# VectorE's order fixed to the program's in the second image's last stage, and sets of convolution weights made in separated places of the first image

## The chip, the cores and the metric

The kernel runs on one core of one Trainium2 chip. The metric is the device time of one execution in microseconds (us). Before the change the median of three runs is 3011.64 us (3008.14 to 3016.84). In the program's names, PE is TensorE (matrix products), DVE is VectorE, ACT is ScalarE, POOL is GpSimd and SP is SyncE, which here only issues transfers (DMAs).

## The reference

Two images of 256 channels and 64 x 64 pixels pass through two layers, each added to its input after a group normalisation:

```python
x = x + _L0_conv_ref(_gn(x), L0_conv_qkv_w, L0_conv_qkv_b, 8)
x = x + _L1_conv_ref(_gn(x), ...)
```

Layer 0 is a plain attention of 8 heads over all 4096 pixels. Layer 1 is what the change touches. From q, k, v (1 x 1 convolutions of its input) it makes two attentions over groups of 64 pixels, one after the other ("lr" with widely spaced pixels, then "sr" with 8 x 8 blocks), and beside them a 3 x 3 convolution; the two results are added with the weights rate1 and rate2:

```python
feats = _bn_relu(_c1x1(ctx, lr_W_w), lr_W_scale, lr_W_shift)
qx = _bn_relu(_c1x1(_bn_relu(_c1x1(feats, sr_fq1_w), ...), sr_fq2_w), ...)
kx = _bn_relu(_c1x1(_bn_relu(_c1x1(feats, sr_fk1_w), ...), sr_fk2_w), ...)
ctx2 = _sa(qx, kx, vx, DH, DW)          # softmax(q k) v within a group of 64
feats2 = _bn_relu(_c1x1(ctx2, sr_W_w), sr_W_scale, sr_W_shift)
out_conv = lax.conv_general_dilated(f_conv, dep_w, (1, 1), ((1, 1), (1, 1)), ...)
return rate1 * out_att + rate2 * out_conv
```

## The kernel before

The program is one function, `direct_layers`, that works through image 0 and then image 1 (`b` is 0 or 1). The 4096 pixels of an image are 8 tiles of 512, and its 256 channels are 2 halves of 128 partitions. For each image come layer 0 (`project0`, `attention0`, most of the time) and then layer 1 in two parts, `layer1_first` (the "lr" attention) and `layer1_second` (the "sr" attention and the 3 x 3 convolution, the last stage of the image).

**The last stage.** `layer1_second` loops over the 8 tiles t. An iteration has, in the program's order: the q branch (`branch`: two products, phq L1582 and prq L1597, each followed by a ScalarE bn_relu, L1341, that makes hq and rq); a convolution step; the k branch in the same way (phk, prk, hk, rk); and `group_attention`: the scores sp (L1276), a softmax, two transposes at (L1308), a copy bd (L1317) and the products pc (L1328), with the values pvs (L1252) between them. The softmax is a chain of short VectorE operations with one exponential on ScalarE in its middle: the maximum nm4 (L1296), the difference e (L1298), the sum den (L1301), its reciprocal (L1302) and the scaled e (L1303). At the end of an iteration stand `conv_edges` (ScalarE, L1218), which corrects the tile's border pixels, and the result's additions. `spots` says which convolution steps lie in which iteration, at three places: 0 after the q branch, 1 within the attention (behind the scores, ahead of at), 2 after the attention.

**A step of the convolution.** The 3 x 3 convolution is done by small transforms, products of transformed weights with transformed pixels, and transforms back. Every call of `conv` makes the *transform* of the next step, col and v, and then runs the *step* itself, products and drain:

- In image 0 (`conv_transform`, `conv_step`, 16 steps (s, q)) GpSimd makes col (L1048) and v (L1052) alone. TensorE makes 32 products mm (L1062). The drain is a copy on ScalarE (L1069) and four VectorE operations z that read mm (L1070 to L1073). Additions into the tiles x follow (L1086, L1090, L1092).
- In image 1 (`wide_transform`, `wide_step`, 12 turns: (0,0) to (0,5), then (1,5) to (1,0)) GpSimd makes the first part of col (L1155), VectorE two scaled additions (L1157) and a last addition (L1160), and then GpSimd makes v in four operations (L1165). TensorE makes 32 products (L1180). The drain is a copy on ScalarE (L1198 for q = 1, L1200 otherwise) and four VectorE operations z (L1201 to L1204). Then 4 or 16 additions into the tiles xphase follow (L1211).

In both cases mm comes from a pool of one buffer (`pacc`), so a group of products can start only when the last drain operation of the group before is done. col has one buffer too.

**The wider weights.** Image 1 needs two more columns of transformed weights than image 0. `wider_weights(wf, r, stage)` makes them from image 0's weights `wf` for one of four rows r, called a set here. A set is four VectorE operations (L1102 to L1105, each 128 x 512) into `stage` and two transfers of 256 KB (L1107, issued by SP) from there to DRAM, from which image 1 loads them. `stage` is one tile, so a set can't be written before the transfers of the set before it are done.

**What sets the order.** Instructions of one engine run in the order in which they are emitted to it. Within `tc.manual_schedule(engines=...)` (L1612) the engines named keep the order of the program text. For the others a scheduler chooses the order by its own estimates of when operands are ready. `tc.issue_after(ins)` holds what is emitted under it behind the instruction `ins` on the engine of `ins` itself. `kept["bd"]` is the last bd copy, a VectorE instruction, and `kept["rows"]` is the last bn_relu of a hidden layer, a ScalarE instruction. `near` is true for the last two iterations of image 0, where TensorE and VectorE both keep the program's order; in all other iterations only TensorE does.

Of the kernel before, what the change touches and what calls it, by code (L numbers as in the profile page):

```python
# [41 lines left out]
def direct_layers(ctx: ExitStack, tc: tile.TileContext, a: dict, out: bass.AP, bad: bass.AP):  # L42
# [17 lines left out]
    def w4(shape, name, dtype=F32):  # L60
        return work.tile(shape, dtype, tag="w4", name=name)

    kept = {}
# [10 lines left out]
    def bank(shape, name, at=None):  # L74
        if at is None:
            at = psum["first"] + psum["turn"] % len(psum["banks"])
            psum["turn"] += 1
        return psum["banks"][at].tile(shape, F32, tag="bank", name=name)
# [52 lines left out]
    for name in ("w1", "w2"):  # L131
        by_out[name] = wpool.tile([P, KC, C], F32, tag="wp", name=f"{name}_by_out")

        for i in range(4):
            r = 64 * (i % 2)
# [63 lines left out]
    for u in range(4):  # L199
        r = HD0 * u  # L200
# [896 lines left out]
    def wider_weights(wf, r, stage):  # L1097

        parts = [stage[:, n, :].rearrange("p (k c) -> p k c", k=KC) for n in range(2)]
        one, two = parts  # L1100
        w = [wf[:, :, 4 * r + q, :] for q in range(4)]
        nc.vector.scalar_tensor_tensor(one, w[3], 4.0, w[0], ALU.mult, ALU.add)  # L1102
        nc.vector.tensor_sub(two, w[1], w[2])
        nc.vector.scalar_tensor_tensor(one, two, 2.0, one, ALU.mult, ALU.add)
        nc.vector.scalar_tensor_tensor(two, two, -4.0, one, ALU.mult, ALU.add)  # L1105
        for n in range(2):
            nc.sync.dma_start(out=wf_more[:, n, :, r, :], in_=parts[n])  # L1107
# [380 lines left out]
    def layer1_second(b, xts, feats, mean, rstd, shift, pacc, following):  # L1488
# [29 lines left out]
        wf = None  # L1518
# [9 lines left out]
        def conv(behind_products=None, behind_drain=None):  # L1528
            nonlocal done, wf
            if wf is None:  # L1530
                wf = fetch_conv_weights(b)
            if done + 1 < len(turns):
                ahead[done + 1] = transform(b, xp, *turns[done + 1])
            additions = step_of(b, xts, wf, ahead.pop(done), *turns[done], pacc, behind_products)
            next(additions)
            held.append(additions)
            if behind_drain:
                behind_drain()
            else:
                while held:  # L1540
                    next(held.pop(0), None)
            done += 1
# [18 lines left out]
        if b:  # L1561
            wf = WideWeights(b)
# [9 lines left out]
        for t in range(NT):  # L1572
            nt = f"sr_{b}_{t}"
            f = [
                feats[k][:, 8 * t : 8 * t + 8].rearrange("p o d e -> p (o d e)") for k in range(KC)
            ]

            def hidden(one, col1, nm):
                hid = w4([P, KC, T], f"h{nm}_{nt}")
                ph = [bank([P, T], f"ph{nm}_{nt}_{m}") for m in range(KC)]  # L1580
                for k, m in ((0, 0), (0, 1), (1, 0), (1, 1)) if t == 0 else ((0, 0), (1, 0), (0, 1), (1, 1)):
                    nc.tensor.matmul(  # L1582
                        ph[m], wts[one][:, k, m * P : (m + 1) * P], f[k], start=k == 0, stop=k == KC - 1
                    )
                    if k == KC - 1:
                        kept["rows"] = bn_relu(hid[:, m, :], ph[m], col1, m)
                return hid

            def branch(one, two, col1, col2, nm, between=None):
                hid = hids.pop(nm, None) or hidden(one, col1, nm)  # L1590
                if between:
                    between()
                res = w4([P, KC, T], f"r{nm}_{nt}")
                pr = [bank([P, T], f"pr{nm}_{nt}_{m}") for m in range(KC)]
                for k in range(KC):
                    for m in range(KC):
                        nc.tensor.matmul(  # L1597
                            pr[m], wts[two][:, k, m * P : (m + 1) * P], hid[:, k, :], start=k == 0, stop=k == KC - 1
                        )
                for m in range(KC):  # L1600
                    bn_relu(res[:, m, :], pr[m], col2, m)
                return res

            E = mybir.EngineType
            seam = b == 0 and t == NT - 1
            near = b == 0 and t >= NT - 2

            def step(n=1):
                for _ in range(n if near else 0):
                    next(then)  # L1610

            with tc.manual_schedule(engines={E.PE, E.DVE} if near else {E.PE}):  # L1612
                hids = {}
                if t == 0:
                    hids = {"q": hidden("fq1", V_FQ1, "q"), "k": hidden("fk1", V_FK1, "k")}
                q = branch("fq1", "fq2", V_FQ1, V_FQ2, "q")
                if pending:
                    next(pending)
                    next(pending, None)
                    pending = None  # L1620
                with tc.issue_after(kept["rows"].ins):
                    for tt in images.get(t, ()):
                        to_image(tt)
                if 0 in spots.get(t, ()) and (b or t > 2):
                    conv(step if seam else None)
                if seam:
                    for n in sorted(results):
                        give(n)
                k = branch("fk1", "fk2", V_FK1, V_FK2, "k", step if seam else None)
                in_x = b and t % 4 == 0  # L1630
                res = xpool.tile([P, KC, T], F32, tag="x", name=f"res_{nt}") if in_x else w4([P, KC, T], f"res_{nt}")

                def to_res(m, pc, res=res):

                    bn_relu(
                        res[:, m, :].rearrange("p (d o e) -> p o d e", d=8, o=8),
                        pc.rearrange("p (o d e) -> p o d e", o=8, d=8), V_SRW, m,
                    )

                parts = group_attention(  # L1640
                    nt, q, k, lambda c, w, f=f: f[c][:, w * P : (w + 1) * P], wts["fv"], to_res, apart=t + 1 < NT,
                    split=t + 1 == NT, fill=lambda m: step(3 if seam else 0),
                )
                if seam:
                    step(5)
                if b == 0 and t == 2:
                    conv(behind_drain=lambda: next(parts))
                else:
                    next(parts)
                step()  # L1650
                if 1 in spots.get(t, ()):
                    conv(None if t < 2 and b == 0 else lambda: next(parts))
                elif b or t > 1:
                    next(parts)
                if t < 2 and b == 0:
                    pending = parts
                else:
                    if seam:
                        step(2)
                    next(parts, None)  # L1660
                    if seam:
                        for _ in then:
                            pass
                if 2 in spots.get(t, ()):
                    conv(step)
            if b == 0 and t == 1:


                with tc.issue_after(kept["seam"]):
                    kept["bias"] = conv_weights()  # L1670
                with tc.issue_after(kept["made"].ins):
                    for k in range(KC):
                        nc.vector.memset(xp[:, k, 0, :], 0.0)
                ahead[0] = conv_transform(b, xp, *turns[0])
            for tt in ((), (0, 1))[t] if b == 0 and t < 2 else (t,):
                conv_edges(xts, tt)
            if b == B - 1 and t == 2:
                report()
            results[t] = res
            if b:  # L1680
                for m in range(KC):
                    nc.vector.tensor_scalar(res[:, m, :], res[:, m, :], wts["rate1"], None, ALU.mult)
            if b == 0 and t in (3, 4):
                if t == 3:
                    stage = xpool.tile([P, KC, T], F32, tag="x", name="stage")
                with tc.issue_after(kept["bd"].ins):
                    for r in range(2 * (t - 3), 2 * (t - 3) + 2):
                        wider_weights(wf, r, stage)
            for n in sorted(n for n in results if done >= (NQ * (n // 4 + 1) if b else 4 * (n // 2 + 1))):
                give(n)  # L1690
            if b == 0 and t == NT - 3:
                next(then)
# [625 lines left out]
```

## Time and profile before

| what | value |
|---|---|
| median of three runs | 3011.64 us (3008.14, 3011.64, 3016.84) |
| the profiled execution's own time | 3011.38 us |
| its span | 3009.5 us, 63901 instructions |
| mean TensorE clock granted | 0.995 of full speed |
| the part of image 0's last stage with the sets and the steps around them | about 1360 to 1480 us |
| last stage of image 1, with its convolution steps | about 2740 to 3009 us |

The profile is one execution; times in it count from the start of its span. A row of the timeline gives start, length, engine, line of the kernel, operation, and output tile <- input tiles; "x32" says that 32 instructions in a row are shown as one, and the brackets at the end give the idle time before them and what ended it. A row of the waits gives who waited <- for whom: the sum in us, the number of times, and the longest. A row of the windows gives a stretch, its length, the busy time and number of operations of PE, PE's weight loads, DVE, ACT and POOL, then the granted TensorE clock, the share of the DMA engines and GB/s. Matmuls are pipelined, so their lengths overlap a little.

### The profile page before, as it was taken

The page shows a single profiled execution, that of the slowest core. Times are in us where ns is not written, and L with a number is a line of the kernel's source. Part 1 is how long each engine was busy: PE and PEld are TensorE (multiplying, and loading weights), DVE is VectorE, ACT ScalarE, POOL GpSimd, SP SyncE. Part 2 cuts the span into 40 slices and gives each one's busy share as a digit, 9 for nine tenths or more (in the row PEclk, how much of TensorE's full clock was granted, in tenths as well). Part 3 has the DMA queues.
Part 4 walks back from the last instruction along what each step waited for, and adds up shares of the span by engine and source line. Part 5 has one row for each costly group of instructions (what it writes and reads, how often), then busy time and mean ns, then how long its engine had stood idle before and what let it go on. Part 6 is the DMA issues. An engine that isn't in the chain of part 4 may idle for free.

```text
span 3009.5 us, 63901 instructions
## 1 busy us (share of the span) xinstructions
PE 2945.0 (98%) x25043; PEld 1830.7 (61%) x25043; DVE 2499.7 (83%) x3196; ACT 2336.1 (78%) x3283; POOL 815.0 (27%) x910
## 2 busy tenths in 40 slices
PE   7999999999999999998999999999999999998998
PEld 4555556665565656676765565566655656566665
DVE  4698998999899999956655989989998989955874
ACT  2699999999999994532235999999999999943433
POOL 1022222322222221065400232223222222213430
PEclk9999999999999999999999999999999999999999
DMA  7979778897888761231249797788978877720010
GB/s 257 277 139 184 148 157 168 160 190 149 164 181 161 154 145 43 62 139 64 63 171 264 147 182 146 163 166 162 187 147 170 176 156 151 154 69 22 15 57 30
DMA packets 254660, 431.82 MB, mean 143 GB/s; under 512 B 99416, under 2 KB 118668, under 8 KB 252172
## 3 DMA queue, kind: packets, MB, share of 16 engines
q0 software_dynamic: 96960, 237.57, 41.2%
q1 hardware_dynamic: 157244, 189.81, 23.1%
q8 instruction: 198, 3.24, 0.4%
q14 instruction: 114, 0.93, 0.1%
q10 hardware_dynamic: 144, 0.26, 0.0%
HBM read 124.27 MB, written 70.48 MB: 65 GB/s over the span
## 4 chain that ended last, share of the span: by engine, by line
PE 86%; DVE 6%; DMA 4%; ACT 2%; POOL 1%; issue 1%; SPq 0%; ACTq 0%; POOLq 0%; DVEq 0%
PE ring L594 32%; PE av L609 30%; PE mm L1062 3%; PE mm L1180 3%; PE p_wk L457 2%; PE p_wq L457 2%; DVE prep L984 2%; PE pv L483 2%; PE prq_sr L1597 1%; PE prk_sr L1597 1%; PE phk_sr L1582 1%; PE phq_sr L1582 1%; PE pvs_sr L1252 1%; DMA acc<-v 1%; PE ring L609 1%; PE pvs_lr L1252 1%
## 5 line engine op out<-in xcount | busy, mean ns | idle before, releaser
L600 ACT ACTIVATE es<-ring 128x512 f32<-128x512 f32 (+2 forms) x1574 | 1201.5, 906 | 35.8 <-PE ring L594 21.3
L594 PE MATMUL ring<-q,k 128*128 128x512 f32 x4096 | 1082.8, 407 | 7.9 <-ACT es L600 5.1
L646 DVE TENSOR_TENSOR e<-e,es 128x1024 f32<-128x1024 f32 (+1 forms) x942 | 1029.0, 1153 | 28.5 <-ACT es L600 27.0
L594 PEld LDWEIGHTS ring<-q,k 128*128 128x128 f32 x4096 | 731.3, 188 | 382.6 <-ACT es L600 116.8
L600 ACT ACTIVATE v<-ring 128x512 f32<-128x512 f32 (+2 forms) x1036 | 785.1, 892 | 17.2 <-PE ring L594 7.7
L609 PE MATMUL av<-es,v 128*32 128x256 f32 (+1 forms) x9648 | 722.5, 389 | 0.0
L646 DVE TENSOR_TENSOR e<-e,v 128x1024 f32<-128x1024 f32 (+1 forms) x624 | 669.1, 1128 | 15.5 <-ACT v L600 15.0
L609 PE MATMUL av<-v 128*32 128x256 f32 x6224 | 506.1, 389 | 0.0
L609 PEld LDWEIGHTS av<-es,v 128*32 128x32 f32 x9648 | 325.1, 109 | 263.3 <-issue 104.5
L609 PEld LDWEIGHTS av<-v 128*32 128x32 f32 x6224 | 222.2, 109 | 169.9 <-issue 70.4
L656 POOL DMA_DIRECT2D es<-es x116 | 99.0, 854 | 442.1 <-ACT es L600 419.1
L656 POOL DMA_DIRECT2D acc<-es x126 | 126.8, 1011 | 130.6 <-ACT es L600 42.9
L654 POOL DMA_DIRECT2D es<-es x20 | 11.4, 570 | 495.3 <-ACT es L600 390.0
L656 POOL DMA_DIRECT2D es<-v x74 | 63.3, 856 | 291.0 <-ACT v L600 259.4
L1062 PE MATMUL mm<-v,wf 128*128 128x256 f32 x512 | 118.2, 391 | 10.6 <-DVE z L1073 10.6
L656 POOL DMA_DIRECT2D v<-es x114 | 116.2, 1019 | 25.6 <-ACT es L600 12.2
L1062 PEld LDWEIGHTS mm<-v,wf 128*128 128x128 f32 x512 | 99.5, 196 | 28.7 <-issue 14.5
L656 POOL DMA_DIRECT2D acc<-v x86 | 88.2, 1026 | 83.6 <-DMA acc<-es 37.8
L1052 POOL TENSOR_TENSOR v<-col 128x512 f32<-128x512 f32 x64 | 83.6, 1334 | 88.3 <-DVE x L1086 33.9
L1180 PE MATMUL mm<-v,wf 128*128 128x256 f32 x384 | 85.6, 381 | 2.6 <-issue 2.6
L984 DVE SCALAR_TENSOR_TENSOR prep<-prep 128x256 f32<-128x256 f32 x198 | 83.6, 477 | 0.4
L1165 POOL TENSOR_TENSOR v<-col 128x512 f32<-128x512 f32 x48 | 59.9, 1282 | 86.1 <-DVE col L1160 86.1
(281 smaller groups left out, 2790.2 us busy)
## 6 DMA issues: line engine op xcount, KB each, us to landing
acc<-es POOLq DMA_DIRECT2D x122, 512.0 KB, 6.2
acc<-v POOLq DMA_DIRECT2D x78, 512.0 KB, 6.4
es<-es POOLq DMA_DIRECT2D x136, 256.0 KB, 4.0
v<-es POOLq DMA_DIRECT2D x134, 256.0 KB, 5.2
k<-wk_halves SPq DMA_DIRECT2D x64, 512.0 KB
q<-wq_halves SPq DMA_DIRECT2D x256, 128.0 KB
v<-v POOLq DMA_DIRECT2D x88, 256.0 KB, 5.0
es<-v POOLq DMA_DIRECT2D x86, 256.0 KB, 4.2
```

Source lines behind the costliest of these rows:

```text
L457: made = nc.tensor.matmul(pq, w0[nm][:, k, g * P : (g + 1) * P], xn[:, k, n], start=k == 0, stop=k == KC - 1)
L483: nc.tensor.matmul(pv[:, j, :], xn[:, k, n0 : n0 + P], w0["wv0"][:, k, :], start=k == 0, stop=k == KC - 1)
L594: touch(nc.tensor.matmul(sc[:, i, :], held["k", g // 2][:, j * P : (j + 1) * P], held["q", g, u // 2][:, u % 2, :], start=True, stop=True, ...
L600: nc.scalar.activation(dst, sc, AF.Exp, scale=SC0), set(range(at % BANKS, at % BANKS + m))
L609: note(nc.tensor.matmul(dst[HD0 * u : HD0 * u + HD0, n], lhs, rhs(u)[:, n], start=start, stop=stop))
L646: nc.vector.tensor_add(dst[:, s, :], dst[:, s, :], src)
L656: nc.gpsimd.dma_start(out=dst, in_=src, accum_op=ALU.add)
L984: nc.vector.scalar_tensor_tensor(acc, src, s, acc, ALU.mult, ALU.add)
L1052: (nc.gpsimd.tensor_add if plus else nc.gpsimd.tensor_sub)(dst, rows(one), rows(two))
L1062: nc.tensor.matmul(mm[:, m, r, :], wf[:, k, 4 * r + q, m * P : (m + 1) * P], v[r // 2][:, r % 2, k, :], start=k == 0, stop=k == KC - 1,)
L1180: nc.tensor.matmul(mm[:, r, :, m, :], wide.of(q)[:, k, r, m * P : (m + 1) * P], v[r // 2][:, r % 2, k, :], start=k == 0, stop=k == KC - 1,)
L1252: nc.tensor.matmul(pv[:, i, :], tokens(c, 2 * half + i), wv[:, c, :], start=c == 0, stop=c == KC - 1)
```

## The change

Two things are changed in `layer1_second`. First, the iterations of image 1 now name VectorE beside TensorE in `tc.manual_schedule`, so that VectorE keeps the program's order there. Second, the four sets of wider weights: before, sets 0 and 1 were emitted after iteration t = 3 of image 0 and sets 2 and 3 after t = 4, each pair behind the last bd copy. Now sets 0, 1 and 2 are emitted after t = 3, 4 and 5, one each, behind the bd copy; set 3 is emitted within iteration t = 5, behind the step at place 0, under `tc.issue_after(kept["rows"].ins)`.

```diff
-            with tc.manual_schedule(engines={E.PE, E.DVE} if near else {E.PE}):
+            with tc.manual_schedule(engines={E.PE, E.DVE} if near or b else {E.PE}):
...
                 if 0 in spots.get(t, ()) and (b or t > 2):
                     conv(step if seam else None)
+                if b == 0 and t == 5:
+                    with tc.issue_after(kept["rows"].ins):
+                        wider_weights(wf, 3, stage)
...
-            if b == 0 and t in (3, 4):
+            if b == 0 and 3 <= t < 6:
                 if t == 3:
                     stage = xpool.tile([P, KC, T], F32, tag="x", name="stage")
                 with tc.issue_after(kept["bd"].ins):
-                    for r in range(2 * (t - 3), 2 * (t - 3) + 2):
-                        wider_weights(wf, r, stage)
+                    wider_weights(wf, t - 3, stage)
```

The first part adds and removes no instruction. The second keeps the sixteen VectorE operations and eight transfers and changes only where they stand.

## The prediction

> **What bounds the kernel now.** I read the page first, then TensorE's waits and timeline in the two places the diff touches, then the engines they wait for.
>
> ```profile
> PE 2945.0 (98%) x25043; PEld 1830.7 (61%) x25043; DVE 2499.7 (83%) x3196; ACT 2336.1 (78%) x3283; POOL 815.0 (27%) x910
> ...
> PE 86%; DVE 6%; DMA 4%; ACT 2%; POOL 1%; issue 1%; SPq 0%; ACTq 0%; POOLq 0%; DVEq 0%
> ```
>
> TensorE is busy 98% of the span and is 86% of the chain that ends last. The change moves work on VectorE, so it can only alter the few waits TensorE still has. The views of its waits, over 1340 to 1540 us (first image) and 2740 to 3010 us (second image):
>
> ```profile
> PE mm L1062 <- DVE z L1073: 9.6, 2, 7.0
> ```
> ```profile
> PE at_sr L1308 <- DVE e_sr L1303: 3.7, 1, 3.7
> PE mm L1180 <- issue: 2.6, 1, 2.6
> ```
>
> Its timeline shows the four (idle before, in brackets):
>
> ```profile
> 1381.03 8.83 PE L1062 MATMUL mm<-v,wf 128*128 128x256 f32 x32 [2.60 <-DVE z L1073]
> ...
> 1431.19 9.94 PE L1062 MATMUL mm<-v,wf 128*128 128x256 f32 x32 [7.04 <-DVE z L1073]
> ...
> 2769.59 0.69 PE L1308 MATMUL at_sr<-ident,e_sr 128*128 128x128 f32 x2 [3.74 <-DVE e_sr L1303]
> ...
> 2779.56 7.14 PE L1180 MATMUL mm<-v,wf 128*128 128x256 f32 x32 [2.60 <-issue]
> ```
>
> A group of 32 products undisturbed takes 7.07 (1366.21); at 1381 it took 8.83, at 1431 9.94. The stretches behind three of the idles say why; PEclk is the third figure from the end:
>
> ```profile
> 1381.00:1384.00 3.00, 2.97 (x10) 2.51 (x11) 2.99 (x11) 0.50 (x3) 0.00 (x0) 0.71 0.00 0
> 1431.00:1434.00 3.00, 2.81 (x7) 2.30 (x8) 1.89 (x8) 0.57 (x2) 1.03 (x1) 0.50 0.45 162
> 2769.50:2772.00 2.50, 2.41 (x7) 2.05 (x8) 2.46 (x5) 0.00 (x0) 1.12 (x1) 0.50 0.11 46
> ```
>
> So an idle costs itself and then some: 2.60+1.76=4.4 at 1381 (4.54 by the starts of neighbouring groups), 7.04+2.87=9.9 at 1431, 3.74+2.6 at 2769. After 2779 the clock stayed at 1.00. The price of half rate is thus 0 to 2.9.
>
> VectorE around the last one:
>
> ```profile
> 2778.14 0.73 DVE L1157 SCALAR_TENSOR_TENSOR col<-col,xp 128x544 f32<-128x544 f32 x1 [4.59 <-POOL col L1155]
> 2778.78 0.68 DVE L1204 TENSOR_TENSOR z<-z,mm 128x512 f32<-128x512 f32 x1
> ...
> 2803.10 8.13 DVE L1211 SCALAR_TENSOR_TENSOR xphase<-z,xphase 128x256 f32<-128x256 f32 x16
> ...
> 2924.34 5.54 DVE L1211 SCALAR_TENSOR_TENSOR xphase<-z,xphase 128x256 f32<-128x256 f32 x16
> ```
>
> The last drain of mm into z (L1204) stood behind a col operation that waited 4.59 for GpSimd; "issue" is really this, because the products share one PSUM tile. And the same 16 additions take 8.13 beside GpSimd's v and col (2798.93 to 2806.3), 5.54 without it: operations with two SBUF inputs advance about one per GpSimd operation (1.27 each). Drains from PSUM keep their 0.7.
>
> **First image: the sets.** A set is four operations L1102–1105 (0.69 each) and two transfers on SP. Before, two sets stand back to back at A (after t=3, mm at 1381) and at B (after t=4, mm at 1431); the second set of each waits for the first's transfers (1.57 at 1375.24). By the built order of the changed program, A keeps one set; B still has two, sets 1 and 3, since the wait on kept["rows"], a ScalarE result, does not hold VectorE's operations; the third place (C, after t=5) gets set 2. That is three places, not four.
> A: VectorE's first set ends at 1373.67, z then at about 1376.9, before TensorE is ready (1378.26): −4.5, all of it unless z is 1.4 later. The next claimant is mm itself, so no later wait is in sight.
> B: same sequence, 0; bounds −10 (sets fall apart in time) to +1.
> C: L1102 goes between L1070 and L1071 of the z at 1459.05 and is held by GpSimd's v until about 1460.6, so z ends 1.07 later, 0.4 past TensorE's readiness; the remaining three come before the z at 1470.12, done by about 1474.2 against 1475.3. Take +0.4 (0 to 2).
> SP: the two transfers of set 3 now stand ahead of one x load of the next image, needed far later; 0. Were that load wanted at once, it would come one write later; the nearest row for such a hold is the 1.57 that set waits for set, and none of TensorE's waits is on SP.
> Sum −4.1 (−14 to −1).
>
> **Second image: VectorE in program order.** The softmax chain (L1296–1303) now precedes the column operations (L1157, L1160) of the next turn, but the first or first two L1157 of each turn after that are still ahead of the drains' end: in program order transform(next) stands before the step of this turn. So the long wait goes, and each drain can wait for GpSimd anew. From the rows, with T the start of a turn's products when attention follows: softmax begins T+0.12; col on VectorE 2.36 later (2940.76 to 2943.22, less the overlap); GpSimd's v 2.76 after col begins (2828.83 to 2831.58); the next col 5.07 after v (2831.58 to 2836.65); its end 2.23 on. Thus the next L1157 may run at T+12.54, whereas the drain is ready at T+8.3.
> *Start.* mm_0_0 at 2758.68; e is done by 2761.3, so at follows at once (3.74+2.6 gone), and mm_0_1 starts at 2770.28 for 2779.56. But v for the second turn begins only at 2763.92, the third col gates VectorE (additions held, col 2772.55–2775.53), GpSimd's next col ends 2782.88, and the drain between ends 2788.23: mm_0_2 at 2788.35 for 2792.55, though TensorE is ready at 2783.2. Gain 4.2, of which a new idle of 5.15 is already taken off; its clock costs +2.6 (1.7 to 2.9, between the 1381 and the 1431 row). Net −1.6.
> *t=2.* The wait for rk (0.5 in all) goes: −0.5. The drain of mm_0_3 waits for L1157 until T+12.54, its additions start T+16.05, the edge operations (ScalarE, L1218) need the fifth of them at T+17.9, and in ScalarE's new order hq's second half now stands behind an edge pair. Before, hq did too, as here, but the additions were in time:
>
> ```profile
> 2822.63 0.49 ACT L1218 ACTIVATE xphase<-xphase,edges 128x8 f32<-128x8 f32 x2
> 2823.53 0.51 ACT L1218 ACTIVATE xphase<-xphase,edges 128x8 f32<-128x8 f32 x2 [0.41 <-DVE xphase L1211]
> 2823.95 0.76 ACT L1341 ACTIVATE hq_sr<-phq_sr,vecs 128x512 f32<-128x512 f32 x1
> ```
>
> hq ends T+19.07; prq's second half wants it at T+15.9: +3.25, clock +1.3 (0 to 2.6).
> *t=3.* Same shape at mm_0_5, two more additions needed: hq T+18.6 against T+16.46: +2.15, clock +0.5 (0 to 1.8).
> *t=4, 5.* The additions of turn (1,3) run beside v and col, so the softmax of t=4 begins 3.6 late (38.0 against 34.4 after turn (1,4) starts). The 7.1 of products cover that, but bd, which now follows col on VectorE, comes 0.8 late. The additions of turn (1,2) are held the same way, their first and fourth feed the edges ahead of hq of t=5, and prq waits 3.9: +4.7, clock +2.0 (0 to 2.6).
> *From t=6* no column work is left: 0; if a drain slipped past its 1.3 cover it would cost below 1.
> Sum: −1.6−0.5+4.55+2.65+6.7 = **+11.8**; the bounds are −9.5 (3.74, 2.62, 2.60 and 0.5 gone, nothing new) and +16 (every clock price at its upper end, 15.3, and 1 from t=6).
>
> [...] The idle of 2.60 at 1378.4 left 0.71 of the clock and lost 1.8, that of 3.74 left 0.50. [...]
>
> **Sum.** The profiled execution took 3011.38 (span 3009.5), 0.26 under the median 3011.64. 3011.38 −4.1 +11.8 = **3019.1**.
>
> **Rivals.**
> *New waits cost the full price* (slower): at each of the four new idles (mm_0_2, prq of t=2, 3 and 5) half rate costs 2.87 as at 1431, 11.5 for the 6.4 taken: 3024; with one wait's delay handed to the next, up to 3029. For: the new idles exceed 2 us each. Against: after 2779 it cost nothing. It decides once three of the four cost over 2.
> *The waits don't form* (not slower): one mechanism, GpSimd's col. If it is done by T+9 in place of T+12.5, the drains are not held, the last three waits fall away and 3005 remains (−4.1 −2.1); with the idle before mm_0_2 gone too, 2997.8 (−4.1 −9.5). For: col takes only 2.2 and before the change it was done long ahead. Against: v of 5.0 stands in front of it, and v waits for VectorE's col, which now comes after softmax.
> *The sets truly come apart*: B's 10 goes too, 3009 with the second image as summed. Against: the built order has them adjacent. That A's gain does not appear (change without effect there) would give 3011.38 +0.4 +11.8, 3024.
>
> **How the numbers follow.** The waits form about as summed: 0.50, own range 3013 to 3025, 0.28 of it within 0.3% (9 us, about what a measurement tells from no change), 0.22 above. Full price or more, or A without gain: 0.26, slower. Waits don't form: 0.17, 0.08 same and 0.09 faster. Sets apart: 0.07, same. So faster 0.09, same 0.43, slower 0.48. The range of 3005 to 3027 leaves out the 2998 end and the top of the full-price case, two in ten.
>
> **What would show it.** Right: no wait at the first image's mm after t=3; still about 7 before the one after t=4; no wait at the first at of the second image; a wait of about 5 at mm_0_2 with L1157 ahead of a drain; prq waits of 2 to 4 on hq, released by additions. Wrong: VectorE's L1157 never waiting for GpSimd in front of a drain, or ScalarE running hq ahead of the edges.

## The result and the profile after

The changed kernel takes 3017.17 us (median of 20 runs, 3013.75 to 3020.14), the kernel before 3011.54 us (20 runs, 3008.14 to 3016.84). The ratio is 1.0017 with a 95% interval of 1.0010 to 1.0023, so the change costs between 3 and 7 us. The forecast was 3019.1. The profiled execution of the changed kernel took 3017.19.

Its page, two lines:

```profile
span 3015.7 us, 63901 instructions
...
PE 2947.1 (98%) x25043; PEld 1829.6 (61%) x25043; DVE 2505.7 (83%) x3196; ACT 2336.2 (77%) x3283; POOL 815.8 (27%) x910
```

The busy times have hardly moved. What moved are TensorE's waits. The view of its waits over the same stretches as before, first image and second image (without two of 0.2 in the second):

```profile
PE mm L1062 <- DVE z L1073: 7.0, 1, 7.0
```
```profile
PE prq_sr L1597 <- ACT hq_sr L1341: 8.3, 3, 3.5
PE mm L1180 <- POOL v L1165: 5.2, 1, 5.2
```

Of the four waits before, three are gone (2.6 in the first image, 3.7 and 2.6 in the second). Four new ones stand in the second image, and the wait of 7.0 is untouched. TensorE's timeline:

```profile
1379.87 7.07 PE L1062 MATMUL mm<-v,wf 128*128 128x256 f32 x32
...
1428.28 9.99 PE L1062 MATMUL mm<-v,wf 128*128 128x256 f32 x32 [7.05 <-DVE z L1073]
...
2762.67 0.38 PE L1308 MATMUL at_sr<-ident,e_sr 128*128 128x128 f32 x2
...
2785.49 8.83 PE L1180 MATMUL mm<-v,wf 128*128 128x256 f32 x32 [5.15 <-POOL v L1165]
...
2822.99 3.54 PE L1597 MATMUL prq_sr<-hq_sr,wt_fq 128*128 128x512 f32 x4 [3.01 <-ACT hq_sr L1341]
...
2861.56 1.98 PE L1597 MATMUL prq_sr<-hq_sr,wt_fq 128*128 128x512 f32 x4 [1.82 <-ACT hq_sr L1341]
...
2932.31 5.40 PE L1597 MATMUL prq_sr<-hq_sr,wt_fq 128*128 128x512 f32 x8 [3.52 <-ACT hq_sr L1341]
```

The wait of 5.15 is put down to GpSimd's v, which had ended at 2777.6. The drain on VectorE had not. VectorE's timeline of the changed kernel shows it, and then the drain at t=2 and the additions at t=5:

```profile
2779.91 1.36 DVE L1157 SCALAR_TENSOR_TENSOR col<-col,xp 128x544 f32<-128x544 f32 x2 [7.15 <-POOL col L1155]
...
2784.55 0.69 DVE L1204 TENSOR_TENSOR z<-z,mm 128x512 f32<-128x512 f32 x1
...
2816.51 0.72 DVE L1157 SCALAR_TENSOR_TENSOR col<-col,xp 128x544 f32<-128x544 f32 x1 [3.58 <-POOL col L1155]
2817.15 0.68 DVE L1202 TENSOR_TENSOR z<-z,mm 128x512 f32<-128x512 f32 x1
...
2925.97 9.10 DVE L1211 SCALAR_TENSOR_TENSOR xphase<-z,xphase 128x256 f32<-128x256 f32 x16
```

At 2779.91 the column operation of the next iteration had waited 7.15 for GpSimd, and the drain behind it ended only at 2785.24, a quarter of a microsecond ahead of the products. At 2816.51 the same operation stands between the first and the second drain operation. At 2925.97 nothing waits in the queue, but the sixteen additions take 9.10 beside GpSimd's v and col, against 5.54 alone. GpSimd's timeline there:

```profile
2922.49 5.20 POOL L1165 TENSOR_TENSOR v<-col 128x512 f32<-128x512 f32 x4 [9.69 <-DVE col L1160]
2927.78 2.66 POOL L1155 TENSOR_TENSOR col<-xp 128x1088 f32<-128x1088 f32 x1
```

ScalarE's timeline of the changed kernel shows how that reaches prq at t=2, and at t=5 in the last row:

```profile
2821.77 0.51 ACT L1218 ACTIVATE xphase<-xphase,edges 128x8 f32<-128x8 f32 x2 [4.34 <-DVE xphase L1211]
2822.18 0.76 ACT L1341 ACTIVATE hq_sr<-phq_sr,vecs 128x512 f32<-128x512 f32 x1
...
2931.09 0.50 ACT L1218 ACTIVATE xphase<-xphase,edges 128x8 f32<-128x8 f32 x2 [3.33 <-DVE xphase L1211]
```

hq's second half stood behind a border correction that waited 4.34 for an addition; at t=5 both halves stood behind one that waited 3.33.

The gains and losses by place, from the starts of groups of products in the two profiled executions (us, minus is faster):

| place | forecast | measured |
|---|---|---|
| A, products after t=3 of the first image | −4.5 | −4.52 |
| B, products after t=4 | 0 | +0.07 |
| C, products after t=5 | +0.4 | +0.27 |
| second image, first to fourth turn's products | −1.6 | −2.28 |
| t=2, wait for rk | −0.5 | −0.51 |
| t=2, prq | +4.55 | +4.97 |
| t=3, prq | +2.65 | +1.92 |
| t=4 and 5 | +6.7 | +5.59 |
| from t=6 | 0 | 0.00 |
| sum | +7.7 | +5.5 |

The spans differ by 6.2, and 0.7 of it is not in the table. The changed kernel was already 1.6 late ahead of place A, 0.8 of it in the wait for the first transfer (14.9 for 14.1); it regained 0.4 between place C and the second image's first products, and 0.5 behind the last pc. What the change moves lies outside these stretches.

### The profile page after: what moved, and what is told of

Same layout as the page of the kernel before. It is cut to its first block, busy times and chain, and to the rows that moved or that the text cites. A ratio compares the mean times of both kernels' runs of the same rounds, so it can differ in the third digit from the quotient of the medians.

```text
span 3015.7 us, 63901 instructions
## 1 busy us (share of the span) xinstructions
PE 2947.1 (98%) x25043; PEld 1829.6 (61%) x25043; DVE 2505.7 (83%) x3196; ACT 2336.2 (77%) x3283; POOL 815.8 (27%) x910
## 5 line engine op out<-in xcount | busy, mean ns | idle before, releaser
L1062 PEld LDWEIGHTS mm<-v,wf 128*128 128x128 f32 x512 | 98.5, 194 | 26.1 <-issue 12.5
L1180 PEld LDWEIGHTS mm<-v,wf 128*128 128x128 f32 x384 | 73.7, 194 | 18.3 <-POOL v L1165 6.0
```

The lines of the kernel that those rows point to most:

```text
L1062: nc.tensor.matmul(mm[:, m, r, :], wf[:, k, 4 * r + q, m * P : (m + 1) * P], v[r // 2][:, r % 2, k, :], start=k == 0, stop=k == KC - 1,)
L1180: nc.tensor.matmul(mm[:, r, :, m, :], wide.of(q)[:, k, r, m * P : (m + 1) * P], v[r // 2][:, r % 2, k, :], start=k == 0, stop=k == KC - 1,)
```

## The experiments

Two lengths are used below to compare profiles: I, from the products of step (1,0) to those of step (3,0) in the first image, and II, from the first turn's products to the last pc of the second image. Before: I 121.5, II 239.6. Changed: I 117.3, II 249.3. Times and ratios are against runs of the kernel before on the same chip.

### One part alone: the sets

Only the second part of the change is made; line 1612 is left as before (`{E.PE, E.DVE} if near else {E.PE}`).

> Only the sets are moved; VectorE's order in the second image's last stage is left as in the kernel before. My theory (the two parts act in separate places and add up): 4.2 us faster than before (-4.5 at the products after t=3, +0.1 after t=4, +0.3 after t=5), about 3007.4, with the 7 us wait after t=4 still there and the second image's waits of 3.7 and 2.6 back. Rival (the gain in the first image is handed on to a later wait, or the two parts depend on each other): within 1.5 us of before.

Measured: 3008.81 against 3010.73, ratio 0.9994 (0.9985 to 1.0003). I is 116.5, II 239.7: the wait of 2.6 is gone, the 7.0 is there, the second image is as before. The interval reaches from 4.5 faster to 0.9 slower and so does not tell the theory from the rival. The same kernel was run once more:

> The first kernel of this study once more, only the sets moved, to narrow its interval (1.9 faster, between 4.5 faster and 0.9 slower). My theory (the wait of 2.6 goes; its clock costs between 0 and 1.8 from one execution to the next): 2.5 to 4.5 faster than before, 3 to be named. Rival (the gain is given back in the first image): under 1.5 faster.

Measured: 3007.68 against 3013.71, ratio 0.9986 (0.9977 to 0.9995), that is 1.5 to 6.9 faster, about 4, where the first run had about 2. The rival, under 1.5, stands at the very edge of this interval, so it is unlikely but not excluded; the forecast of 4.1 lies in both intervals. In the profiles, I is 116.5 and 116.0 for 121.5.

### The other part alone: the order

```diff
-            with tc.manual_schedule(engines={E.PE, E.DVE} if near else {E.PE}):
+            with tc.manual_schedule(engines={E.PE, E.DVE} if near or b else {E.PE}):
```

> Only VectorE's order is fixed; the sets stay in their two pairs. My theory: 9.7 us slower than before, about 3021.2: the gains of 16 at the start of the second image's last stage are outweighed by waits of 5.2 at the third turn's products, 3.0 and 1.8 at prq of t=2 and 3, and 3.5 at prq of t=5, each with up to 1.8 of lower clock behind it. Rival (the changed kernel's loss comes in part from the sets): below 3018.

Measured: 3020.87 against 3010.73, ratio 1.0040 (1.0028 to 1.0052). II is 249.7, 10.1 longer than before, with waits of 5.13, 3.01, 1.80 and 3.51. The loss lies wholly in this part. Within the intervals the two parts add up: this loss is 8 to 16, the gain of the sets about 2 and 4, and the whole change costs 3 to 7. This run also gave a surprise in the first image, where nothing had been changed. The view of the windows, over the first 3 us behind the wait of 2.61 (2.60 before), of this kernel:

```profile
1381.00:1384.00 3.00, 2.98 (x14) 2.66 (x15) 2.98 (x11) 0.52 (x3) 0.00 (x0) 1.00 0.00 0
```

The clock stayed at 1.00, where the profile before had 0.71 after the same wait, and the products behind it took 7.14 for 8.83. I is 119.1 in place of 121.5 with the same instructions. The price of this idle, 0.07 in one execution and 1.76 in the other, is not a constant of the program.

### The border corrections out of hq's way

```diff
+                if b and t == 0:
+                    with tc.issue_after(kept["rows"].ins):
+                        for tt in range(1, 5):
+                            conv_edges(xts, tt)
...
-            for tt in ((), (0, 1))[t] if b == 0 and t < 2 else (t,):
+            for tt in () if b and 0 < t < 5 else ((), (0, 1))[t] if b == 0 and t < 2 else (t,):
                 conv_edges(xts, tt)
```

> The changed kernel, with the border corrections on ScalarE (L1218) of tiles 1 to 4 of the second image emitted in iteration 0 in place of iterations 1 to 4; VectorE's instruction order is the changed kernel's. My theory (the three prq waits come about because hq's bn_relu stands behind border corrections that wait for late additions): all three waits go, 5.0+1.9+5.4 with their clock, so 12.3 faster than the changed kernel, about 3004.9; the wait of 5.2 at the third turn's products stays. Rival (prq waits because ScalarE or the products' results themselves are late, whoever stands before): the waits stay, 3017.

Measured: 3007.05 against 3010.73, ratio 0.9984 (0.9975 to 0.9992): 3.7 faster than before, where the changed kernel was 5.6 slower, so 9.3 for the 12.3 expected. II is 237.9, 11.3 shorter than the changed kernel's. Of TensorE's waits in the second image, only one is over 0.2:

```profile
PE mm L1180 <- POOL v L1165: 5.1, 1, 5.1
```

All three prq waits are gone while VectorE runs the very same order: a late drain or late additions cost TensorE nothing there as long as nothing of ScalarE's waits for them ahead of hq. Most of the 1.0 that II falls short of the forecast lies in the products behind the 5.13, which took 9.68 here, 8.83 in the changed kernel's profile.

### The columns held behind the drain

```diff
-        nc.vector.tensor_sub(z1, z1, products(3))
+        kept["drain"] = nc.vector.tensor_sub(z1, z1, products(3))
...
-                ahead[done + 1] = transform(b, xp, *turns[done + 1])
+                with tc.issue_after(kept["drain"].ins) if b and done else ExitStack():
+                    ahead[done + 1] = transform(b, xp, *turns[done + 1])
```

> The changed kernel, with each turn's column operations of the second image held behind the last drain operation (L1204) of the turn before on VectorE. My theory (what delays is that L1157 of the next iteration is let in ahead of a drain and waits there for GpSimd): the wait of 5.2 at the third turn's products goes with its clock (6.9), the prq waits of t=2 and 3 shrink to about 1 and 0 (5.6), that of t=5 stays at 3.5; 12.5 faster than the changed kernel, 3004.7. Rival (the additions beside GpSimd's work make the prq waits, the drains' delay doesn't): only the 6.9, 3010.3.

Measured: 3008.33 against 3010.73, ratio 0.9991 (0.9982 to 0.9999); II is 240.8, 8.5 shorter than the changed kernel's and not 12.5. The wait of 5.15 is gone, the products there take 7.07 again, and the wait at t=3 is 0.24. But prq of t=2 waits 4.04, more than before the edit, and that of t=5 2.30. VectorE and ScalarE at t=2 of this kernel:

```profile
2811.65 0.72 DVE L1157 SCALAR_TENSOR_TENSOR col<-col,xp 128x544 f32<-128x544 f32 x1 [3.93 <-POOL col L1155]
2812.29 5.45 DVE L1211 SCALAR_TENSOR_TENSOR xphase<-z,xphase 128x256 f32<-128x256 f32 x16
```
```profile
2814.08 0.51 ACT L1218 ACTIVATE xphase<-xphase,edges 128x8 f32<-128x8 f32 x2 [4.37 <-DVE xphase L1211]
2815.09 0.51 ACT L1218 ACTIVATE xphase<-xphase,edges 128x8 f32<-128x8 f32 x2 [0.50 <-DVE xphase L1211]
2815.50 0.76 ACT L1341 ACTIVATE hq_sr<-phq_sr,vecs 128x512 f32<-128x512 f32 x1
```

The column operation no longer stands ahead of the drain, it stands ahead of the additions, and waits there. The scheduler has also put both pairs of border corrections ahead of hq's second half, where the changed kernel had one. My expectation had the place of the wait right for the drain and missed that it would move one step down the same queue.

### The columns held behind the last addition

The same, with `kept["added"]`, the last addition of the turn before (L1211), in place of the drain.

> The changed kernel, with each turn's column operations of the second image held on VectorE behind the last addition (L1211) of the turn before, not only behind its drain. The run that held them behind the drain still had L1157 wait 3.9 for GpSimd in front of the additions, and the prq wait of t=2 became 4.0. My theory (a wait of L1157 in VectorE's queue delays whatever stands behind it, drain or additions, and the additions hold the border corrections and hq): the waits at the third turn's products and at prq of t=2 and t=3 all go (6.9, 5.0, 1.9), that of t=5 stays at 2 to 3.5, so 13.8 faster than the changed kernel and about 8 faster than before. Rival (the additions are late because they run beside GpSimd, not because of the wait): prq of t=2 still waits over 2, at best 5 faster than before.

Measured: 3004.48 against 3011.16, ratio 0.9975 (0.9966 to 0.9984). That is 6.7 faster than before, for the 8 expected. II is 235.8, 13.5 shorter than the changed kernel's, near the 13.8 expected, but not as expected: prq of t=2 still waits 2.79 and that of t=5 2.11, and the products behind them lost 0.1 each time (1.98 for 1.88 and 3.70 for 3.60). VectorE's additions and GpSimd's work at t=2:

```profile
2807.69 8.73 DVE L1211 SCALAR_TENSOR_TENSOR xphase<-z,xphase 128x256 f32<-128x256 f32 x16
```
```profile
2804.27 5.20 POOL L1165 TENSOR_TENSOR v<-col 128x512 f32<-128x512 f32 x4 [9.76 <-DVE col L1160]
2809.55 2.23 POOL L1155 TENSOR_TENSOR col<-xp 128x1088 f32<-128x1088 f32 x1
```

Nothing waits in VectorE's queue now, and the additions start 4.7 earlier than with the columns held behind the drain (11.8 for 16.5 after that turn's products start), yet they take 8.73 for 5.45. At t=2 the rival is right in the place and not in the price, since the kernel is more than 5 faster than before: the additions are late because of GpSimd, whether they queue behind an operation that waits for it or run beside it. Part of the 2.79 has another cause, though: ScalarE again has both pairs of border corrections ahead of hq's second half, where the changed kernel had one. The first pair starts at 2812.77 and hq at 2814.18; in the changed kernel hq started 0.41 behind the pair, so with one pair ahead prq would have waited about 1.8 here, an estimate from these rows. What GpSimd's v and col cost the sixteen additions is in the rows: 8.73 here and 9.10 at t=5 of the changed kernel beside them, 5.45 without them.

### Both, and then four places for the sets

> The same, and the border corrections of tiles 1 to 4 emitted in iteration 0. My theory (the second image then has none of its waits left): no wait over 0.5 of TensorE in that stage, 19 faster than the changed kernel, 13.5 faster than before. Rival (a new wait takes their place: columns later, so v late for the products two turns on): a wait of mm on v of over 1, less than 10 faster than before.

Measured: 2995.97 against 3011.16, ratio 0.9946 (0.9933 to 0.9960): 15 faster than before, for the 13.5 expected. II is 229.8, 19.5 shorter than the changed kernel's and 9.8 shorter than before. No wait over 0.2 is left of TensorE in it.

The next kernel adds the four places; the set within iteration 5 goes away:

```diff
-                if b == 0 and t == 5:
-                    with tc.issue_after(kept["rows"].ins):
-                        wider_weights(wf, 3, stage)
...
-            if b == 0 and 3 <= t < 6:
-                if t == 3:
+            if b == 0 and 2 <= t < 6:
+                if t == 2:
...
-                    wider_weights(wf, t - 3, stage)
+                    wider_weights(wf, t - 2, stage)
```

> The same, and the four sets emitted after t=2, 3, 4 and 5 of the first image, one each behind the bd copy. My theory (the 7 us wait after t=4 is two sets back to back on VectorE, the second waiting for the first one's transfers): that wait falls to about 1.3, 8 faster than the kernel of the run beside it, about 21 faster than before. Rival (that wait comes from the additions and results beside GpSimd, whatever the sets): it stays above 4, less than 3 faster than the kernel beside it.

Measured: 2990.91 against 3011.16, ratio 0.9932 (0.9918 to 0.9945): 20 us faster than before, the fastest kernel of the study. TensorE's waits in the first image, of this kernel (in the second none is over 0.2):

```profile
PE mm L1062 <- DVE z L1073: 2.3, 1, 2.3
```

The 7.0 has become 2.3. It is not 1.3, since the remaining set, beside GpSimd's work and mixed with the results' additions, still ends at 1418.8. I is 109.8, 6.5 shorter than in the kernel beside it. The gain on that kernel is 5.1 by the medians of five runs each, not 8. To see it alone:

> The changed kernel, its sets alone moved to four places (after t=2, 3, 4 and 5); the second image as in the changed kernel. My theory: the same 8 us as in the run beside it, so about 2.4 faster than before; the second image's waits of 5.2, 3.0, 1.8 and 3.5 stay. Rival (gains in the first image are lost on the way): less than 3 faster than the changed kernel, 2.6 or more slower than before.

Measured: 3011.75 against 3011.16, ratio 1.0001 (0.9991 to 1.0010). I is 111.4, with the same wait of 2.33, but this time the products behind it took 8.83 where the run beside had 7.14. Against the changed kernel's loss of 5.6 it is 5.0 better. Both theory and rival named the wrong size: taking the two sets apart is worth 5. By the timeline the wait that remains stands behind one set and the results' additions beside GpSimd; no run takes these away.

### Program order in the first iteration only

```diff
-            with tc.manual_schedule(engines={E.PE, E.DVE} if near or b else {E.PE}):
+            with tc.manual_schedule(engines={E.PE, E.DVE} if near or (b and t == 0) else {E.PE}):
```

> The changed kernel, with VectorE in program order only in iteration 0 of the second image. From iteration 1 the scheduler again makes columns two turns ahead, as in the kernel before; in program order they are made one turn ahead. My theory (one turn of lead less puts GpSimd's columns and v beside, and L1157 ahead of, each turn's drain and additions; that makes the prq waits): the wait of about 5.2 at the third turn's products stays, the three prq waits fall below 1 each; about 12 faster than the changed kernel, 6 faster than before. Rival (the prq waits follow from the late start alone: the third turn's products are late, so everything behind them is): prq of t=2 still waits over 2, less than 3 faster than before.

Measured: 3008.84 against 3013.71, ratio 0.9986 (0.9977 to 0.9995). TensorE's waits in the second image's last stage:

```profile
PE mm L1180 <- POOL v L1165: 5.2, 1, 5.2
PE at_sr L1308 <- DVE e_sr L1303: 0.9, 1, 0.9
PE prq_sr L1597 <- ACT hq_sr L1341: 0.7, 1, 0.7
```

The 5.2 stays and the prq waits of 3.0, 1.8 and 3.5 shrink to one of 0.74, although the third turn's products come as late as in the changed kernel. So the rival falls. What makes the three waits is program order in the later iterations. By the built order the columns of a turn are then made one turn ahead; in this kernel, from iteration 1 on, they are made two ahead, as before the change. GpSimd's v for the fifth turn shows it, in this kernel and then in the changed one:

```profile
2794.13 5.19 POOL L1165 TENSOR_TENSOR v<-col 128x512 f32<-128x512 f32 x4 [7.38 <-DVE col L1160]
```
```profile
2809.24 4.99 POOL L1165 TENSOR_TENSOR v<-col 128x512 f32<-128x512 f32 x4 [19.00 <-DVE col L1160]
```

The fourth turn's products start at 2801.66 here, 7.5 after that v, and at 2803.93 in the changed kernel, 5.3 before it. The run changes the lead together with everything else that program order fixes, so that the lead alone makes the waits is argued and not shown. II is 241.0, 8.3 shorter than the changed kernel's for the 12 expected: 1.2 of the difference lies in the products behind the 5.2 (10.05, for 8.83), 0.9 the wait at at, 0.7 that at prq, 0.5 one at sp.

## Why the prediction was right

*The sum.* 3019.1 was forecast, 3017.17 measured, inside the range and the likeliest case's own. The direction came from two terms of opposite sign, and each was measured by itself: the sets about −2 and −4 in their two runs (−4.2 by the table's places, forecast −4.1), the order +10.1 (8 to 16 by its interval, forecast +11.8). The forecast gave slower a little more chance (0.48) than no clear change (0.43); the 5.6 measured lies within the 9 us that it counted as no change. That the total came within 2 us is in part luck: the waits were forecast 1.7 too long and their clock 0.9 too dear, and 0.7 the other way came from stretches outside the change's places.

*A, B, C.* Right in place and size. B kept its 7.05: sets 1 and 3 are adjacent on VectorE but for two of the results' additions, and the second waits for the first's transfers. The changed kernel's timeline:

```profile
1417.87 0.68 DVE L1105 SCALAR_TENSOR_TENSOR stage<-stage 128x512 f32<-128x512 f32 x1
...
1419.80 0.68 DVE L1102 SCALAR_TENSOR_TENSOR stage<-wf 128x512 f32<-128x512 f32 x1
1421.64 1.57 DVE L1103 TENSOR_TENSOR stage<-wf 128x512 f32<-128x512 f32 x1 [1.16 <-DMA wf_more<-stage]
```

That answers the rival "the sets truly come apart": they did not, in the change as made. Its price, 10, was too high. When they were taken apart, 5 to 6.5 came back. A's gain came in full, so the case without it falls too.

*The start of the second image.* The wait at at went, and the new idle of 5.15 at the third turn's products came as worked out from the pitches of softmax, col and v, to 0.01. The kernel with the columns held shows its cause: without L1157 in front of the drain it is gone.

*prq of t=2, 3 and 5.* Right in place, and the path over the border corrections to hq is shown by moving them. The waits were 3.01, 1.82 and 3.52 for 3.25, 2.15 and 3.9. (For the first, the forecast's own two times, T+19.07 and T+15.9, differ by 3.17 and not 3.25.) At t=2 the mechanism was only part of it: without L1157 in front, the additions are late beside GpSimd (8.73 for 5.45), and prq still waited 2.79. bd's 0.8 at t=4 hardly showed (0.1), because the softmax there began 2.9 late and not 3.6.

*The clock.* Mis-sized as well, by about half as much as the waits. I took 6.4 in all for half rate behind four idles, after 5.15 a value of 2.6; measured were 1.76 (8.83 for 7.07), 1.84 (1.66 in prq and 0.18 behind it), 0.1 and 1.8, together 5.5. The granted clock over the first 3 us behind the 5.15, the 3.01 and the 3.52 was 0.54, 0.55 and 0.52. These are one execution's: the same idle of 5.15 lost 1.8 to 3.0 in five. The waits under the 6.4 were 1.7 too long (15.3 with bd, for 13.6). From which length on an idle costs clock is not shown: the 3.01 lost as much as the 5.15 (1.84 and 1.76), the 1.82 lost 0.1.

*The rivals.* Full price at each idle (3024) did not come: it needed three of the four idles to cost over 2, and in this profile none did. The waits did form, so 3005 did not come either.

## What to carry to other kernels

Fixing VectorE's order to the program's took away two waits of TensorE (3.7 and 2.6) and brought four others (5.1, 3.0, 1.8 and 3.5): the program's text also says how far ahead work is made, and here, with one turn of lead less, another engine's unfinished work stood in front of short operations that a third engine was waiting for. When a result is late, follow it over all queues: here a small correction on ScalarE, needed by nobody soon, stood ahead of the one operation that TensorE wanted, and moving it was worth 9 to 11 us without touching the engine that was late. Work that is to be separated should be looked for in the built order of the engine that runs it, since here a hold on another engine's instruction did not separate it: on VectorE set 1 begins its last operation at 1417.87 and set 3 its first at 1419.80.

## What was not expected

The price of an idle of TensorE differs between executions of the same instructions. Idle before a group of 32 products of 7.07, and what the group lost:

| idle, us | lost, us |
|---|---|
| 7.04 to 7.05 (ten executions) | 1.6, 1.8, 1.9, 1.9, 2.1, 2.2, 2.2, 2.2, 2.9, 2.9 |
| 5.13 to 5.17 (five) | 1.8, 1.8, 2.3, 2.6, 3.0 |
| 2.60 and 2.61 after t=3 (two) | 1.76 and 0.07 |
| 2.31 and 2.33 after t=4 (two) | 0.07 and 1.76 |
| 2.38, 2.60 and 3.50, some 7 us behind a longer idle (three) | 0.07 each |

What sets the price is not shown. In the pairs at 2.6 and 2.3 the first image's instructions are the same, yet 2.60 and 2.33 lost 1.76 and 2.61 and 2.31 lost 0.07. The idles of 3.74 to 3.77 at the first at of the second image, which stand before other products, lost 2.6, 2.9 and 1.7. For a forecast on this kernel the clock behind an idle of 2 to 4 us (2.31 to 3.77 in these rows) is thus a term of 0 to 2.9 and not a number.
